# Transformer block with routed experts on one core: heads exchanged through DRAM in pairs, two sequences transposed on TensorE, small work moved to GpSimd, a written-out order of steps

## The chip, the cores and the metric

The kernel runs on one core of a Trainium2 chip. The metric is the device time of one execution in microseconds, lower is better. Three timed executions of the kernel before gave 1186.53, 1188.41 and 1190.04 us; the median, 1188.41 us, is its time. One execution was profiled; it took 1186.62 us, and the span from its first to its last instruction is 1184.9 us.

## The reference

The input is 16 sequences of 256 tokens with 256 channels, in float32, and one condition vector per sequence. The block is attention with 16 heads of 64 channels and then 8 experts; each expert takes the 512 tokens (of 4096) that give it the highest gate.

```python
shift = jax.nn.silu(t) @ W_ada.T + b_ada
h = _ln(x, ln1_g, ln1_b) + shift
qkv = (h @ Wqkv.T).reshape(b, n, 3, H, HD)
q = _ln(qkv[:, :, 0].transpose(0, 2, 1, 3), qn_g, qn_b)
k = _ln(qkv[:, :, 1].transpose(0, 2, 1, 3), kn_g, kn_b)
v = qkv[:, :, 2].transpose(0, 2, 1, 3)
attn = jax.nn.softmax(jnp.einsum('bhnd,bhmd->bhnm', q, k) / jnp.sqrt(jnp.float32(HD)), axis=-1)
o = jnp.einsum('bhnm,bhmd->bhnd', attn, v)
x = x + o.transpose(0, 2, 1, 3).reshape(b, n, H * HD) @ Wout.T
tok = x.reshape(-1, d)
gate = jax.nn.softmax(tok @ Wgate.T, axis=-1)
vals, idx = jax.lax.top_k(gate.T, k_cap)
g = _ln(tok[idx_flat], mlp_g, mlp_b).reshape(k_cap, E, d)
y = jax.nn.gelu(jnp.einsum('ked,ehd->keh', g, fc1s) + b1s, approximate=True)
y = (jnp.einsum('keh,edh->ked', y, fc2s) + b2s) * w[..., None]
tok = tok.at[idx_flat].add(y.reshape(-1, d))
```

## The kernel before

**Attention, per sequence.** The kernel is written as steps, small functions that each issue a few instructions on one engine. For every sequence b:

- `First` (L486) normalises x. VectorE takes the statistics (L471, L473) and adds eps (L475), GpSimd raises to the power -0.5 (L181, called `rsqrt`), VectorE applies it (L481). TensorE transposes the result (L505), ScalarE evicts it as hT (L513).
- `Group` (L527) makes 512 columns of q, k or v for 128 tokens: TensorE (L539, 8 groups of q and k and 4 of v per sequence), and for q and k the square on ScalarE (L552), the sum and the eps on VectorE (L556, L560), the power on GpSimd (L181), the scaling on VectorE (L572), four transposes on TensorE (L581) and the eviction on ScalarE (L593). v is copied by ScalarE (L548).
- `Quad` (L601) handles four heads: two pairs i, each with two heads j. `scores` (L614) writes the scores of a pair to PSUM, the two heads in the upper and lower half of TensorE's rows. Then come the maxima on VectorE (L621), the exponentials with their sums on ScalarE (L630), the reciprocal on VectorE (L637), the normalisation on GpSimd (L641). The probabilities must be transposed before the product with v. VectorE transposes blocks of 32x32 (`turn`, L651) into a tile `pb` for four heads; `away` (L659) writes this tile to DRAM in one transfer of 1 MB; `back` (L668) reads it with four transfers of 256 KB, each into 32 partitions, which completes the transposition. `product` (L679) multiplies with v for one pair, and ScalarE evicts both pairs (L690). `pb`, `blocks` (in DRAM) and `prT` have two buffers each.
- `Tail` (L693) projects half a sequence (L701), adds x and takes the statistics of the second normalisation (L708, L471 to L475), stores the token (L712), applies the normalisation (L481) and stores it for the experts (L722), transposes the token (L727) and computes the gate (L738, L744).

**Routing.** When all but the last sequence have their gates, the gates are turned (L803), and a loop of 30 steps finds for each expert the threshold of its first 256 tokens, bit by bit: VectorE compares and counts (L866), TensorE sums the counts over partitions (L875), VectorE decides on the bit (L881, L890). Then follow masks, running sums, places, the turn of the places (L932), their split (L943, L944), one-hot rows (L999 to L1002) and their matmuls into a list of tokens (L1010). GpSimd gathers these tokens (L1026), and the first expert job starts (L1035, L1042, L1054). The last sequence, number 15, is still being worked on meanwhile; its tokens join the second half of the experts' lists.

**Experts.** 16 jobs, each with 256 tokens of one expert: up (L1054), GELU (L1061), down (L1070), scaling (L1081) and a scatter that adds (L1087).

**What sets the order.** All engines work through their own queue in order, and the order in which steps are issued is found when the program is built. Each step has an engine, a duration, what it needs and makes, the tiles that it uses, and a place (`at`, L1098). `Plan.order` (L69 to L139) is a list scheduler: on each engine it takes, of the steps that could start, the one with the lowest place. The places are given by `PLACES` (for sequences 0, 1, 14 and 15, and one list for all others, L258) and `OTHERS` (L357). The exchange is two steps on SP: `away` and, when it has landed, `back`. The experts behind the first job are issued by a loop of their own (L1285), which the change leaves as it is.

```python
plan = Plan(dict(
    mm=3, sc=4, po=1, xs=5, hT=2, qT=2, kT=2, v=2, oT=2, xn=4, sq=2, ss=4, qk=3, nmax=8,
    sums=4, pr=5, pb=2, prT=2, blocks=2, tok=3, tn=2, tokT=2, pa=1, l1=4, l2=4,
))
```

Of the kernel before, what the change touches and what calls it, by code (L numbers as in the profile page):

```python
# [9 lines left out]
F32 = mybir.dt.float32  # L10
# [8 lines left out]
P = 128  # L19
# [25 lines left out]
class Plan:  # L45
# [4 lines left out]

    SWITCH = 0.1

# [9 lines left out]
    def move(self, k, places, base=0.0):  # L65
        for n, p in enumerate(places):
            self.steps[k + n] = (base + p,) + self.steps[k + n][1:]

    def order(self):  # L69
        steps = self.steps  # L70
        waits, after = [0] * len(steps), [[] for _ in steps]
        users, first = {}, {}
        for k, s in enumerate(steps):
            for need in s[4]:
                for m in self.makers[need]:
                    after[m].append(k)
                    waits[k] += 1
            for t in s[5]:
                users[t] = users.get(t, 0) + 1
                first[t] = min(first.get(t, s[0]), s[0])  # L80
        queue, before = {}, {}
        for t in sorted(first, key=lambda t: (first[t], t)):
            q = queue.setdefault(t[0], [])
            before[t] = (q[-1] if q else None, q[-self.bufs[t[0]]] if len(q) >= self.bufs[t[0]] else None)
            q.append(t)
        opened, seen, ready = set(), dict.fromkeys(users, 0.0), [0.0] * len(steps)
        engines = sorted({s[1] for s in steps})
        free, mode, could = dict.fromkeys(engines, 0.0), 0, {e: [] for e in engines}
        for k, s in enumerate(steps):
            if not waits[k]:  # L90
                could[s[1]].append(k)

        def since(k):
            at = ready[k]
            for t in steps[k][5]:
                if t not in opened:
                    last, old = before[t]
                    if (last and last not in opened and last not in steps[k][5]) or (old and users[old]):
                        return None
                    if old:  # L100
                        at = max(at, seen[old])
            return at

        now, begun = 0.0, []
        while any(could.values()):
            soonest = None
            for e in engines:
                best = None
                for k in could[e]:
                    at = since(k)  # L110
                    if at is None:
                        continue
                    at = max(at, free[e])
                    if at > now:
                        soonest = at if soonest is None else min(soonest, at)
                    elif best is None or steps[k][0] < steps[best][0]:
                        best = k
                if best is None:
                    continue
                place, _, took, _, _, tiles, new, lag = steps[best]  # L120
                could[e].remove(best)
                begun.append((now, best))
                if e == "PE" and new != mode:
                    took, mode = took + self.SWITCH, new
                free[e] = now + took
                for t in tiles:
                    opened.add(t)
                    users[t] -= 1
                    seen[t] = max(seen[t], free[e] + lag)
                for j in after[best]:  # L130
                    waits[j] -= 1
                    ready[j] = max(ready[j], free[e] + lag)
                    if not waits[j]:
                        could[steps[j][1]].append(j)
                soonest = now
            assert soonest is not None, "the steps wait for each other"
            now = soonest
        assert len(begun) == len(steps)
        return begun  # L139
# [3 lines left out]
def kernel(  # L143
# [83 lines left out]
    def make_others():  # L227
# [20 lines left out]

    PERIOD = 48.3
# [8 lines left out]
    PLACES = {  # L258
        0: (
            -1144.55, -164.36, -115.53, -130.99, -318.93, -203.16, -250.78, -275.49, -88.56,  # L260
            -92.44, -65.27, -85.65, -66.22, -65.85, -65.32, 12.14, -6.18, -116.86, -181.88,
            -226.33, -125.11, -66.56, 28.05, -105.91, -20.3, -102.65, -221.15, -75.09, 2.35,
            -80.49, 1.34, -67.49, -85.29, 6.61, 41.35, -62.52, -33.41, -103.77, 18.66, -30.22,
            54.18, 129.48, -13.42, -83.84, 39.96, -48.35, -19.59, -36.56, -17.89, -45.17, 55.43,
            -70.52, -11.75, -35.26, 18.2, 127.34, -40.65, 197.67, -41.87, 25.57, -34.78, 6.26,
            -0.72, -16.64, -24.42, -19.76, -33.5, 146.36, -15.21, -80.44, -121.15, 16.4, -39.26,
            141.09, 130.08, -22.71, 7.22, 19.47, -35, 26, -18.23, 114.81, -30.2, 29.23, -17.79,
            38.44, -19.99, 169.58, 80.02, 70.31, -8.6, 150.94, -2.15, 56.48, 101.61, -24.78,
            -6.1, 29.81, -75.75, -44.1, -91.93, -42.35, 8.4, 56.38, -74.75, 9.88, -96.01, 81.36,
            4.1, -11.15, -69.31, 111.09, -81.61, -79.47, 132.37, -55.21, 0.19, -6.58, 10.81,  # L270
            -17.63, -89.05, -107.92, -85.01, 55.81, 73.89, -3.1, 47.74, 73.13, -1.31, 11.3,
            -4.77, -7.89, 119.67, 92.55, 13.36, 18.97, 19.3, 0.26, 98.83, 99.7, 5.08, 90.2,
            98.25, 89.81, 28.34, 13.88, -25.95, 96.99, 23.08, 24.48, 165.57, 95.49, 17.49,
            25.97, 340.13, 17.81, 30.6, 82.65, 76.24, 137.46, 26.87, 119.95, 28.51, 62.39,
            98.03, 29.11, 80.48, 33.67, 134.77, 55.75, 148.81, 19.6, 184.91, 184.91, 71.13,
            145.9, 172.26, -1.27, 65.12, 94.09, 77.65, 61.8, 129.73, 115.28, 77.3, 197, 137.64,
            83.55, 49.39, 91.96, 309.57, 84.45, 103.71,
        ),
        1: (
            -1099.37, -54.3, -64.13, -49.72, 71.37, -53.23, -29.87, -97.99, -83.01, -35.49,  # L280
            -46.75, -34.18, 81.89, -9.83, -37.19, 36.64, -62.82, 55.44, -65.48, -20.12, -47.55,
            -31.78, -47.55, -26.5, -51.81, -65.03, 0.47, 13.43, -46.75, -17.66, -38.8, -69.23,
            -71.58, 29.14, 26.88, -56, -43.27, -44.63, 17.07, -13.08, 26.91, 4.19, 10.21,
            -26.32, 70.91, -27.78, -19.98, -4.95, -12.76, -18.52, 56.95, -24.15, 33.02, -10.4,
            -14.8, 156.65, -25.28, 57.31, -18.9, -26.29, -16.56, -10.04, -7.87, -9.89, -16.41,
            19.91, -19.2, -7.41, 17.97, 72.84, -26.36, 1.28, -2.29, 247.68, 32.65, 5.1, 57.03,
            13.72, 64.3, 1.04, 25.24, 113.13, 73.57, 11.96, 44.14, 13.22, 7.46, 193.37, 89.15,
            25.45, 6.95, 78.59, 27.38, 82.69, 48.92, 27.8, 15.94, 20.2, -8.51, -6.59, 81.43,
            162.24, -3.77, 171.23, -7.27, 83.73, -2.31, 16.51, 10.99, -6.84, 2.75, 0.93, 116.67,
            47.85, 133.75, 4.98, 82.62, 123.39, 75.52, 59.15, 47.91, -25.4, 28.45, 153.76, 17.7,  # L290
            122.51, 20, 152.23, 14.52, 8.47, 137.08, 80.87, 51.01, 31.66, 134.83, 94.03, 23.05,
            126.07, 25.97, 99.38, 24.04, 64.78, 151.81, 126.94, 18.1, 166.1, 24.05, 47.47,
            129.86, 33.28, 68.61, 32.17, 28.96, 32.46, 270.75, 32.53, 67.18, 73.71, 15.97,
            43.31, 38.83, 226.09, 38.38, 44.84, 49.78, 71.7, 36.68, 123.74, 79.99, 76.02,
            102.24, 32.47, 43.7, 280.07, 70.72, 73.86, 167.32, 118.25, 62.67, 75.97, 178.87,
            46.5, 263.88, 75.76, 77.93, 71.3, 272.62, 159.42, 99, 76.57, 183.69, 106.19, 54.29,
        ),
        7: (
            191.51, -163.95, -123.74, -35.99, -95.07, -16.18, -24, -78.96, 25.94, -55.05, 8.08,
            -53.5, -64.73, -0.18, -46.06, 23.75, -54.52, -16.62, -53.05, -52.69, -42.2, 57.54,  # L300
            -48.11, 6.09, -51.7, 54.34, 45.68, -40.43, -29.34, -38.29, 100.8, -47.57, -35.63,
            20.29, -6.51, -31.42, 49.06, 18.7, -41.88, -24.12, 16.51, 24.92, 85.5, -32.56,
# [81 lines left out]
    if True:  # L384
# [80 lines left out]
        class Norm:  # L465
# [11 lines left out]
            def power(self):  # L477
                rsqrt(self.rs[:, 1:2], self.rs[:, 0:1])
# [48 lines left out]
        class Group:  # L527
# [36 lines left out]
            def power(self):  # L564
                rsqrt(self.ss[:, 1, :], self.ss[:, 0, :])
# [811 lines left out]
```

## Time and profile before

| what | value |
|---|---|
| median of three executions | 1188.41 us |
| the profiled execution: its time, its span | 1186.62 us, 1184.9 us |
| busy: TensorE matmul, VectorE, ScalarE, GpSimd | 92%, 68%, 50%, 49% of the span |
| mean granted TensorE clock | 0.965 |
| start of the 30 counts of the first routing (L875), last count | 859.6 us, 907.0 us |
| first block of the first expert job (L1054) | 930.2 us |
| end of TensorE's work | about 1174 us |

The profile lists instructions by engine, kernel line and operation, with the tiles' names as out<-in, a count, the busy time and the mean duration. "PEld" is the weight load of a matmul, which overlaps other matmuls. A number in brackets in the timeline is the idle time of the engine before that row, with what ended it; consecutive equal instructions of a row are merged (x8 is eight instructions). A float32 matmul appears as two instructions. The ends of matmuls are modelled, so for TensorE the distance from start to start says more than the busy time. Times of the timeline count from the span's start.

### The profile page before, as it was taken

What the parts mean: (1) busy time and instruction counts of PE and PEld (TensorE: products, weight loads), DVE (VectorE), ACT (ScalarE), POOL (GpSimd) and SP (SyncE); (2) the same over time, 40 slices, a digit from 0 to 9 for tenths busy, and PEclk for the clock granted to TensorE, in tenths of its full rate; (3) what the DMA queues carried; (4) which work ended last, traced back from release to release, by engine and by line L of the source; (5) the groups of instructions that cost most, each with busy time, mean ns of one, the idle gap of its engine ahead of it and who ended that gap; (6) DMA issues with size and microseconds to landing.
All of it is one profiled execution on the core that took longest, in us unless ns stands there. A gap on an engine that the chain in (4) does not pass through costs nothing. (4 is left out here: it accounts for less than half of the span.)

```text
span 1184.9 us, 17925 instructions
## 1 busy us (share of the span) xinstructions
PE 1089.6 (92%) x5787; PEld 715.9 (60%) x5787; DVE 800.6 (68%) x2364; ACT 593.9 (50%) x1661; POOL 574.8 (49%) x805
## 2 busy tenths in 40 slices
PE   7899999999999999999999999999845799999996
PEld 4444546565565656555565655556624688888885
DVE  6776667676867767676866767578657478755540
ACT  2675556656565666565555655556501333233331
POOL 2665555566656546555655565456400233333332
PEclk8998999999999999999999999999966899999998
DMA  5147356656664647746665664746850366666661
GB/s 197 52 133 219 124 140 204 196 155 169 195 193 136 204 125 222 193 150 177 174 201 165 178 186 138 198 146 207 249 170 10 109 184 183 187 187 187 186 184 22
DMA packets 92813, 196.53 MB, mean 166 GB/s; under 512 B 9008, under 2 KB 45104, under 8 KB 84528
## 3 DMA queue, kind: packets, MB, share of 16 engines
q1 hardware_dynamic: 82944, 183.27, 52.4%
q0 software_dynamic: 6144, 8.39, 3.8%
q10 hardware_dynamic: 3632, 3.74, 0.9%
q8 instruction: 46, 0.75, 0.3%
q14 instruction: 47, 0.39, 0.1%
HBM read 115.67 MB, written 79.69 MB: 165 GB/s over the span
## 5 line engine op out<-in xcount | busy, mean ns | idle before, releaser
L539 PE MATMUL pm<-wq,hT 128*128 128x512 f32 x768 | 363.8, 610 | 5.5 <-DVE wq L461 3.5
L181 POOL TENSOR_TENSOR ss<-ss,neghalf 128x8 f32<-128x8 f32 x128 | 210.0, 1645 | 222.3 <-DVE ss L560 191.0
L641 POOL TENSOR_SCALAR pr<-pr,sums 128x256 f32<-128x256 f32 x512 | 236.3, 479 | 90.7 <-DVE sums L637 85.1
L630 ACT ACTIVATE pr<-sc,nmax 128x256 f32<-128x256 f32 x512 | 236.7, 477 | 44.8 <-DVE nmax L621 41.6
L539 PEld LDWEIGHTS pm<-wq,hT 128*128 128x128 f32 x768 | 139.0, 194 | 145.7 <-issue 125.4
L621 DVE TENSOR_REDUCE nmax<-sc 128x2 f32<-128x512 f32 x256 | 165.4, 677 | 56.2 <-PE sc L614 56.0
L651 DVE STREAM_TRANSPOSE pb<-pr 128x512 f32<-128x512 f32 x256 | 171.7, 690 | 17.1 <-POOL pr L641 16.5
L679 PE MATMUL po<-prT,v 128*64 128x256 f32 x1024 | 135.0, 401 | 38.3 <-DMA prT<-blocks 34.5
L614 PE MATMUL sc<-kT,qT 64*128 64x256 f32 x1024 | 142.2, 400 | 0.1
L679 PEld LDWEIGHTS po<-prT,v 128*64 128x64 f32 x1024 | 73.0, 141 | 105.8 <-issue 33.9
L556 DVE TENSOR_REDUCE ss<-sq 128x8 f32<-128x512 f32 x128 | 86.6, 676 | 56.7 <-ACT sq L552 56.0
L701 PE MATMUL pw<-wo,oT 128*128 128x256 f32 x512 | 120.6, 391 | 0.0
L1054 PE MATMUL ph<-xT,w 128*128 128x256 f32 x512 | 118.3, 384 | 0.0
L614 PEld LDWEIGHTS sc<-kT,qT 64*128 64x128 f32 x1024 | 90.1, 187 | 45.9 <-issue 33.6
L1070 PE MATMUL py<-w,hid 128*128 128x256 f32 x512 | 116.6, 380 | 0.0
L701 PEld LDWEIGHTS pw<-wo,oT 128*128 128x128 f32 x512 | 99.2, 196 | 25.6 <-issue 9.4
L552 ACT ACTIVATE sq<-pm 128x512 f32<-128x512 f32 x128 | 76.7, 600 | 74.4 <-PE pm L539 70.3
L1087 POOL DMA_INDIRECT out<-y,idx x32 | 51.1, 1597 | 120.7 <-DVE y L1081 57.5
L572 DVE TENSOR_TENSOR qk<-pm,ss 128x512 f32<-128x512 f32 x128 | 87.3, 684 | 29.8 <-POOL ss L181 29.3
L630 ACT ACTIVATION_READ_ACCUMULATOR pr<-sc,nmax 128x1 f32 x512 | 107.4, 210 | 0.0
L1054 PEld LDWEIGHTS ph<-xT,w 128*128 128x128 f32 x512 | 96.0, 191 | 13.0
L1070 PEld LDWEIGHTS py<-w,hid 128*128 128x128 f32 x512 | 95.5, 190 | 12.7
(133 smaller groups left out, 1034.0 us busy)
## 6 DMA issues: line engine op xcount, KB each, us to landing
blocks<-pb SPq DMA_DIRECT2D x64, 1024.0 KB, 4.3
prT<-blocks SPq DMA_DIRECT2D x256, 256.0 KB, 6.5
w<-in_fc2T SPq DMA_DIRECT2D x16, 1024.0 KB, 5.5
w<-in_fc1T SPq DMA_DIRECT2D x16, 1024.0 KB, 8.3
out<-tok SPq DMA_DIRECT2D x32, 128.0 KB, 5.0
xn_dram<-tn SPq DMA_DIRECT2D x32, 128.0 KB, 4.1
xs<-in_x SPq DMA_DIRECT2D x12, 256.0 KB, 3.0
b<-in_b2s SPq DMA_DIRECT2D x16, 128.0 KB, 8.4
```

The lines of the kernel that those rows point to most:

```text
L181: nc.gpsimd.tensor_tensor(dst, src, neghalf[:, : src.shape[1]], ALU.pow)
L539: nc.tensor.matmul(self.pm, hTs[self.b][:, c, bass.ts(self.t, P)], wq[:, c, bass.ts(self.g, GW)], start=(c == 0), stop=(c == DC - 1),)
L572: engine.tensor_tensor(self.qk.rearrange("p (h d) -> p h d", d=HD), src.rearrange("p (h d) -> p h d", d=HD), self.ss[:, 1, :].unsqueeze(2) ...
L614: nc.tensor.matmul(self.sc[i, j][:, t, :], qTs[self.b][rows, hp, bass.ts(t, P)], kTs[self.b][rows, hp, :], start=True, stop=True,)
L621: nc.vector.tensor_reduce(self.nmax[i, j], self.sc[i, j], AX.X, ALU.max, negate=True)
L630: nc.scalar.activation(self.pr[i, j][:, t, :], self.sc[i, j][:, t, :], AF.Exp, bias=self.nmax[i, j][:, t : t + 1], scale=1.0, accum_out=se ...
L641: nc.gpsimd.tensor_scalar(self.pr[i, j][:, t, :], self.pr[i, j][:, t, :], self.sums[i][:, 1, j, t : t + 1], 1.0, ALU.mult, ALU.mult,)
L651: nc.vector.transpose(self.pb[:, :, :, 2 * i + j].rearrange("p k c t n -> p t c k n"), self.pr[i, j].rearrange("p t (c k m) -> p t c k m", ...
L679: nc.tensor.matmul(self.po[j * HD : (j + 1) * HD, i, :], vs[self.b][:, c, bass.ts(4 * self.d + 2 * i + j, HD)], self.prT[:, :, c, 2 * i + ...
L701: nc.tensor.matmul(self.pw, oTs[self.b][:, hp // 2, self.t, hp % 2, :], wo[:, hp, :], start=(hp == 0), stop=(hp == HP - 1),)
L1054: nc.tensor.matmul(self.ph[f], self.w1[:, c, bass.ts(f, P)], self.xT[:, c, :], start=(c == 0), stop=(c == DC - 1),)
L1070: nc.tensor.matmul(self.py[i], self.hid[:, f, bass.ts(i, P)], self.w2[:, f, :], start=(f == 0), stop=(f == FC - 1),)
```

## The change

Five things change together.

1. The exchange through DRAM is done for two heads (one pair i) at a time: `pb`, `blocks` and `prT` belong to a pair, with 3, 4 and 4 buffers. `away` writes 512 KB, and each of the four transfers of `back` reads 128 KB, in pieces of 256 floats where there were 512.
2. Sequences 0 and 15 (`DIRECT`) do not go through DRAM: TensorE transposes the probabilities of a head in four 128x128 blocks into a PSUM tile (tag `sc`), and ScalarE copies them to `prT`. VectorE's block transposes fall away for these two.
3. eps is added on GpSimd instead of VectorE (both normalisations, and q and k), and both normalisations are applied on GpSimd.
4. The first job's one-hot rows, 30 in all, go to VectorE, GpSimd and ScalarE as 15, 10 and 5, where they went to VectorE and ScalarE as 20 and 10. `pr` has six buffers instead of five.
5. The scheduler is removed. `PLACES` is now one list with a number for each of the 3669 steps, in the order of the `at` calls, and steps are issued in ascending order of it.

```diff
-    def order(self):
-        steps = self.steps
...
+    def order(self, places):
+        assert len(places) == len(self.steps)
+        return sorted(range(len(places)), key=lambda k: (places[k], k))
...
+    DIRECT = (0, B - 1)
+    PRB = 6
...
+    PLACES = (
+        0, 0, 3.3, 5.22, 3.75, 4.72, 4.42, 7.47, 0.23, 0.53, 9.39, 8, 20.02, 16.58, 12.59, 11.2,
...
-                nc.vector.tensor_scalar_add(self.rs[:, 0:1], self.mv[:, 1:2], EPS)
 
             def power(self):
+                nc.gpsimd.tensor_scalar(
+                    self.rs[:, 0:1], self.mv[:, 1:2], EPS, 1.0, ALU.add, ALU.mult
+                )
                 rsqrt(self.rs[:, 1:2], self.rs[:, 0:1])
 
             def apply(self, dst):
-                nc.vector.tensor_scalar(
+                nc.gpsimd.tensor_scalar(
                     dst, self.src, self.mv[:, 0:1], self.rs[:, 1:2], ALU.subtract, ALU.mult
                 )
...
-                nc.vector.tensor_scalar(
+
+            def power(self):
+                nc.gpsimd.tensor_scalar(
                     self.ss[:, 0, :], self.ss[:, 0, :], 1.0 / HD, EPS, ALU.mult, ALU.add
                 )
-
-            def power(self):
                 rsqrt(self.ss[:, 1, :], self.ss[:, 0, :])
...
-            def away(self):
-
-                self.blocks = dram.tile([QB, SQ, QB, GW], F32, tag="blocks", bufs=2, name="blocks")
+            def away(self, i):
+
+                self.blocks[i] = dram.tile([QB, SQ, QB, N], F32, tag="blocks", bufs=4, name="blocks")
                 nc.sync.dma_start(
-                    self.blocks.rearrange("k m q n -> (k m) (q n)"),
-                    self.pb.rearrange("p q c h t n -> p (q c h t n)"),
-                )
...
+            def turned(self, i):
+                if i not in self.prT:
+                    self.prT[i] = work.tile([P, 2 * TB * N], F32, tag="prT", bufs=4, name="prT")
+                return self.prT[i]
+
+            def back(self, i):
+
+                prT = self.turned(i).rearrange("p (k n) -> p k n", k=QB)
                 for q in range(QB):
                     nc.sync.dma_start(
...
+                        prT[bass.ts(q, SQ)], self.blocks[i][:, :, q].rearrange("k m n -> m k n")
+                    )
+
+            def transposes(self, i, j):
+                self.pp[i, j] = ps.tile([P, TB, N], F32, tag="sc", bufs=4, name="pp")
+                for c in range(TB):
+                    for t in range(TB):
+                        nc.tensor.transpose(
+                            self.pp[i, j][:, c, bass.ts(t, P)],
+                            self.pr[i, j][:, t, bass.ts(c, P)], ident,
+                        )
+
+            def copy(self, i, j):
+                prT = self.turned(i).rearrange("p (h c n) -> p h c n", h=2, c=TB)
+                nc.scalar.copy(prT[:, j], self.pp[i, j])
...
+                    elif engine is nc.gpsimd:
+                        nc.gpsimd.tensor_scalar(
+                            self.oh[:, t, :], lane1, place, 1.0, ALU.is_equal, ALU.mult
+                        )
...
-            sums=4, pr=5, pb=2, prT=2, blocks=2, tok=3, tn=2, tokT=2, pa=1, l1=4, l2=4,
+            sums=4, pr=PRB, pb=3, prT=4, blocks=4, tok=3, tn=2, tokT=2, pa=1, l1=4, l2=4,
...
+            who = "DPADPD" if n == 0 else "DDDDDD"
...
-        for _, k in plan.order():
+        for k in plan.order(PLACES):
             plan.steps[k][3]()
```

What the list says, read off by sorting it. The places of a step on SP or another engine count against TensorE's only through what it needs. On TensorE, behind the gate of the second half of sequence 14, the order is: two products of sequence 15, two of its transposes (a transposes step is one head), the turn of the gates, and then, between the counts of the routing loop (numbered from 29 down to 0):

```
turn of the gates | transposes, scores | count 29 | product, scores, product | 28 | transposes | 27 | - | 26 |
scores, transposes, product | 25 | transposes | 24 | - | 23 | transposes, transposes | 22 |
product, transposes | 21 | transposes, product | 20 | product | 19 | - | 18 | projection | 17 |
projection | 16 | token transposes, gate, token transposes | 15 | gate | 14 | ... | 0
```

Before, the profile has six of the eight products of sequence 15, two of its v groups (L539) and its two projections in or next to this loop; the second projection starts at 912.1 us, behind it. A piece of SP's new order (sequence, then quad and pair as two digits): away 7.11, back 7.11, away 7.20, away 7.21, back 7.20, away 7.30, back 7.21, two stores, away 8.00, away 7.31, a load, a store, away 8.01, back 7.31, back 7.30, a store, back 8.00, back 8.01, away 8.10, back 8.10. Each `back` is four issues.

## The prediction

> **What bounds the kernel now.** I began with the page's 40 slices, to see where TensorE is not full.
>
> ```profile
> PE   7899999999999999999999999999845799999996
> PEclk8998999999999999999999999999966899999998
> ...
> q1 hardware_dynamic: 82944, 183.27, 52.4%
> ...
> q10 hardware_dynamic: 3632, 3.74, 0.9%
> ```
>
> TensorE is nearly full except in the first slices and in three near 70%. The table of busy time by stage puts numbers on this (columns: span, then PE, PEld, DVE, ACT and POOL busy with instructions, TensorE clock, DMA share, GB/s).
>
> ```profile
> 0.00:100.00 100.00, 83.97 (x341) 46.78 (x341) 70.05 (x154) 51.14 (x136) 50.63 (x72) 0.90 0.45 138
> ...
> 182.00:707.00 525.00, 503.13 (x2560) 298.42 (x2560) 380.35 (x849) 314.83 (x921) 304.93 (x455) 1.00 0.63 178
> ...
> 853.00:930.00 77.00, 37.72 (x197) 24.02 (x194) 45.87 (x240) 12.04 (x37) 12.58 (x24) 0.68 0.43 131
> 930.00:1174.00 244.00, 243.63 (x1565) 213.73 (x1563) 140.82 (x766) 80.34 (x165) 80.19 (x66) 1.00 0.55 161
> ```
>
> From 182 to 707 us the projection of a sequence (L701) starts ten times, so a sequence takes 52.5 us. DVE is busy 72%, ACT 60%, POOL 58%, the DMA engines 63%: TensorE is the bound, and only its own work and its own waits matter. Its work, start to start in the timeline of one period: 12 q/k/v blocks at 1.72, 8 blocks of q/k transposes at about 0.5, 8 of scores at 1.06, 4 pairs of products at 1.88, 2 projections at 3.5, the rest 2.1; together 49.8 us. So some 2.7 us of a period are waits. Next I read the waits of TensorE from 125 to 850 us, then the timeline of one period, where they stand at two places:
>
> ```profile
> PE po L679 <- DMA prT<-blocks: 22.4, 19, 1.8
> ```
>
> ```profile
> 430.42 1.95 PE L679 MATMUL po<-prT,v 128*64 128x256 f32 x16 [1.42 <-DMA prT<-blocks]
> ...
> 434.95 1.08 PE L679 MATMUL po<-prT,v 128*64 128x256 f32 x8 [0.93 <-DMA prT<-blocks]
> ```
>
> The product waits for probabilities that come back from DRAM. In the start the same wait costs more, as the clock falls too; at the end it holds up the routing loop (TensorE's timeline, then VectorE's):
>
> ```profile
> 89.97 3.68 PE L679 MATMUL po<-prT,v 128*64 128x256 f32 x16 [3.17 <-DMA prT<-blocks]
> 94.40 3.68 PE L679 MATMUL po<-prT,v 128*64 128x256 f32 x16 [0.76 <-ACT oT L690]
> ...
> 880.74 1.97 PE L679 MATMUL po<-prT,v 128*64 128x256 f32 x8 [5.20 <-DMA prT<-blocks]
> ...
> 895.41 6.48 PE L701 MATMUL pw<-wo,oT 128*128 128x256 f32 x16
> ```
>
> ```profile
> 859.85 0.22 DVE L890 SCALAR_TENSOR_TENSOR cand<-pc,drop,keep 128x1 f32<-128x1 f32 x1 [3.79 <-PE pc L875]
> ...
> 882.87 0.22 DVE L890 SCALAR_TENSOR_TENSOR cand<-pc,drop,keep 128x1 f32<-128x1 f32 x1 [6.39 <-PE pc L875]
> ```
>
> The loop of 30 counts runs from 856 to 907 us. Undisturbed it needs 1.00 us a turn (counts at 864.61 and 865.61), in which TensorE is idle 0.84. It is late where its count stands in TensorE's queue behind a block of sequence 15. From 930 us TensorE is full; the change does not touch that stage.
>
> **The sum**, against the profiled execution (1186.6 us; the median of the three runs is 1.8 above).
>
> *Steady stretch.* Four heads make one 1 MB transfer out (4.3 us to landing) and four of 256 KB back (6.5), and the way out waits for the last of four block transposes. For the wait at 430.42 above, SP's timeline has the way out issued at 416.92 and the ways back from 422.74 on: 13.5 us from the way out to the product. With two heads, the way out waits for two transposes, and there are three, four and four buffers of half the size instead of two. From the scores to the second transpose the rows give two maxima (0.68), two exponentials (1.0), the reciprocal (0.17), two normalisations (0.94) and two transposes (0.69), 6.8 us and with queueing some 10; the exchange adds at most 4.3 + 4 x 0.43 + 6.5 = 12.5. In the list at least 27 us of TensorE work stand between the scores of two heads and their product in sequences 2 to 13 (36 now, but for four heads). Waits before products from 125 to 850 us are 24.6 us by the waits view (22.4, and 1.4 and 0.8 named for ACT), with 0.07 more at each of 21 starts: 26. I take 21 out and leave 5 for new waits. Bounds: +5 (none of the old ones goes and the new ones come on top) and -26. **-21**.
>
> *Sequence 0.* No way through DRAM: the waits of 3.17 and 0.76 go, and the two products of 3.68 at a low clock come back to 1.88: 7.5 us. TensorE also waits 6.2 us there for VectorE's scaling; VectorE loses 16 transposes of 0.69 (11 us) in this stretch, so I take half, 3. Bounds: 1 (next sentence) and 19 (all 16 us that TensorE is idle in the first 100, and 3.5 of the low clock). **-10.5**. ACT pays with 16 copies like L690's (0.59, 9.4 us) where it is busy 51%; that hides, and if it did not, the products would wait for up to 9 us: 10.5 - 9.4 = 1.
>
> *Added TensorE work.* Each of 32 heads is four 128x128 transposes, a block like L581's (0.49). For sequence 0: 16 x 0.49 = 7.8. For sequence 15, ten of 16 stand in the routing window (below), six before: 2.9. Two v blocks of sequence 15 (3.4) now stand ahead of the window, three score blocks (3.2) move into it. The list changes between the score or product form and others 14 times more (335 against 321), at 0.09 each: 1.3. **+12.2**.
>
> *Routing window.* Now: last gate of sequence 14 at 851.4, first expert block at 930.2, 78.8 us. After: 4.6 to the first count, 30 turns of 1.00, plus what the blocks between two counts exceed 0.84. In the list these are 2.96 (product, scores, product), 2.5, 0.98, 1.44, 1.44, 0.95, twice 3.5 (projections) and 1.1; the excess is 10.9, and 0.7 before the turn of the gates: 46.2, against 55.6 now. Full clock is assumed; TensorE is busier here than now, but if the clock fell to half as in 895.41, the blocks would double and 10 us come back. Behind the last count nothing of sequence 15 is left, and a third of the one-hots goes to GpSimd: ten at 0.54 (the nearest row is L207's, 128x128) and 0.9 for the gives, 7.0 to the list, against 9.3 now. That is 2.3 less; bounds +1 and -4. **-11.7**.
>
> *At nothing.* The eps operations (192) and both normalisations (64) go to GpSimd. The trace has no eps there; by its rows a small operation takes 0.23 (L786, 128x16) to 0.56 (L181, 128x1), so 44 to 108 us in all, I take 44, the plain arithmetic; 64 x 0.48 for applying (L641's form) makes 75. GpSimd rises from 58% to 66%, VectorE falls by 62 us. A chain gets 0.2 longer, covered by the blocks that stand between a q/k block and its transposes; without that cover it is 0.2 on each of 128 transposes, 26 us. SP issues 40 instead of 20 exchange transfers a sequence at 0.43 each: 17 of 50 us. SP works in order: a way back that waits for its way out holds the next way out and the stores behind it, and only products and the reuse of token tiles wait for those.
>
> *Packets.* The way back now moves 1 KB instead of 2 KB at a time. The trace's packet records have 2 KB on this path at 152 ns (19.5 us per sequence and engine) and 1 KB elsewhere at 46 to 54; the page's q10 row is 47. Bounds for a 1 KB packet are thus 46 and 152; I take 76, half of the same path's row, so the engines carry what they carry now (32.4 us of a period).
>
> "DMA: Bandwidth & Descriptors" in the Trainium skill (Anatomy of one DMA; Bandwidth) speaks against the change: a transfer costs a fixed 2 us plus its bytes at 436 GB/s, and should be batched to 1 MB or more. By it the way out is 4.4 us (the row: 4.3) and a half of it 3.2, so two in a row take 2.0 longer than one; over 56 quads that is 112 us of an in-order queue, which would make the time 1289 (1186.6 - 10 for the other terms + 112) if TensorE stood behind all of it. The row of TensorE's waits says that it stands behind 24.6 us in all.
>
> Sum: -21 - 10.5 + 12.2 - 11.7 = -31, so 1155.6 in the profiled execution, which lies 1.8 below the median; I give **1156**.
>
> **Rivals.**
> *More than that* (1140): each term at its better end, -26 - 19 + 12.2 - 13.4 = -46. For it: the first two stand on waits that rows name. Against: a new order always brings some wait.
>
> *The waits only move* (1180): two thirds of the steady 21 stay, because SP's queue is in order and has twice the transfers, and the window's clock falls, +10: -31 + 14 + 10 = -7. The change then does not do what it says. For it: SP already waits 104.8 us for the way out to land (L668). Against: in the list other issues stand between most ways out and their ways back.
>
> *Slower* (1207): 1 KB packets cost as much as 2 KB ones. Then the way back takes 4096 x 152 / 16 = 39 us per sequence instead of 19.5, and the engines carry 52 us. No row of the stages has them over 0.63; at 0.95 a sequence takes 54.7, and 14 x 2.2 = 31 come on top, the steady 21 are not won, the rest gives 10. It decides from about 147 ns: then 12.9 + 37.6 = 50.5 us of transfers need a period of 53.2, which eats those 10. For it: 2 KB takes 152 on this path and 84 on q10, so something other than bytes counts. Against: 8 KB takes 317, which goes by bytes.
>
> **How the numbers follow.** Forecast 0.55, more 0.15, waits move 0.20, slower 0.10. The second rival is faster by 7 us in its middle, and 0.3% (about what a measurement can tell from no change) is 3.6, so 0.03 of it lies within; of the slower case 0.01. Faster 0.55 + 0.15 + 0.17 = 0.87, the same 0.04, slower 0.09. The range from 1134 to 1182 takes in the first three cases to their middles and beyond, and leaves out the slower one and the far half of the second rival.
>
> **What would show it.** Right: waits of L679 for DMA under 5 us from 125 to 850; a period near 50; counts of the routing loop about 1 us apart after the projections; no wait of sequence 0's products for DMA. Wrong: 1 KB packets over 130 ns and a DMA share over 0.85; q/k transposes (L581) waiting for GpSimd's chain; the loop longer than 50 us.

## The result and the profile after

After: 1144.41 us (median of four, 1144.07 to 1145.36) against 1188.34 us for before on the same chip; the ratio is 0.9632, interval 0.9615 to 0.9649. The profiled execution took 1144.71 us, its span is 1143.0 us: 41.9 us less than the profiled execution of before, where the prediction had 31 less (its 1156 is the profiled execution's figure, 1155.6; with the 1.8 that it names itself the median's would be 1157).

First the page of the kernel after: the 40 slices of TensorE and of its clock, then the exchange's queue (packets, MB, share of 16 engines).

```profile
PE   6999999999999999999999999999961999999996
...
PEclk7999999999999999999999999999985899999999
...
q1 hardware_dynamic: 117504, 166.51, 45.6%
```

TensorE is now full from the second slice on, one hole is left, the routing window. The queue moves more packets in a smaller share of time, and 9% fewer bytes (166.51 MB instead of 183.27), as two sequences no longer pass through it. The table of busy time by stage of the kernel after (span, then PE, PEld, DVE, ACT and POOL, clock, DMA share, GB/s):

```profile
0.00:100.00 100.00, 89.58 (x408) 50.49 (x408) 52.30 (x103) 57.64 (x146) 68.60 (x108) 0.93 0.20 68
...
180.00:684.00 504.00, 501.15 (x2570) 295.21 (x2568) 345.96 (x685) 313.94 (x922) 378.94 (x616) 1.00 0.58 182
...
822.00:888.00 66.00, 33.57 (x263) 24.33 (x262) 46.45 (x239) 17.99 (x52) 25.59 (x44) 0.72 0.14 47
888.00:1133.00 245.00, 244.60 (x1547) 214.09 (x1547) 140.09 (x762) 79.59 (x162) 80.79 (x66) 0.99 0.55 161
```

Ten sequences take 503.0 us from projection to projection, 50.3 each instead of 52.5; GpSimd is busy 75% of that, the DMA engines 0.58 instead of 0.63. The waits of TensorE from 125 to 822 us in the kernel after, complete (us in total, times, longest):

```profile
PE pq L712 <- DVE qk L703: 2.8, 7, 0.5
PE po L831 <- DVE gates L900: 1.1, 2, 0.8
```

Of the 22.4 us in which products waited for DMA nothing is left. In TensorE's timeline of the window (after), the counts are L1031, the projections of sequence 15 L857, the first expert block L1214:

```profile
824.40 0.18 PE L1031 MATMUL pc<-cnt,twice 128*128 128x1 bf16 x1
...
841.08 3.70 PE L857 MATMUL pw<-wo,oT 128*128 128x256 f32 x16
844.62 0.17 PE L1031 MATMUL pc<-cnt,twice 128*128 128x1 bf16 x1
...
865.27 0.16 PE L1031 MATMUL pc<-cnt,twice 128*128 128x1 bf16 x1 [0.84 <-DVE reach L1022]
...
887.59 2.93 PE L1214 MATMUL ph<-xT,w 128*128 128x256 f32 x6
```

No scores or products of sequence 15 wait for their data between the counts; the loop takes 40.9 us from first to last count instead of 47.4. So what the prediction named as signs of being right is there: no product waits for DMA anywhere in the trace of after, the period is 50.3, and behind the second projection and the two gates the counts stand 1.00 apart (864.27, 865.27). Of its signs of being wrong the trace has one in small: the q/k transposes wait 2.8 us.

For the rest I cut every trace at the same four points of TensorE: first projection of sequence 1, first projection of sequence 11, turn of the gates, first expert block. "Start" ends at the first, then come "ten periods", "run-down" and "window"; what follows, to the end of TensorE's work, is 245 to 247 us in every run. TensorE's work in a stage is the sum of its instructions at the start-to-start interval that each form has where nothing waits (0.429 us for 512 columns, 0.2155 for 256, 0.1075 for a score or product, 0.109 for a transpose, 0.09 per change of form; smaller forms likewise); the remainder is stall. It holds more than waits: 19.1 us in the ten periods of after, where the waits view names 2.8. It also holds what TensorE loses where its granted clock is below 1 (0.93 before and 0.96 after up to some 180 us, 0.68 and 0.72 in the window, by the stage rows). So only its changes are read.

| | start | ten periods | run-down | window |
|---|---|---|---|---|
| before: length, work | 182.4, 139.5 | 524.9, 484.4 | 146.2, 134.9 | 76.7, 20.6 |
| after: length, work | 180.8, 153.1 | 503.0, 483.9 | 138.7, 133.6 | 65.0, 24.7 |
| change of the stall | -15.2 | -21.4 | -6.2 | -15.8 |

The work grows by 15.9 us, the stall falls by 58.6, and the first expert block starts 42.6 earlier (930.2, 887.6).

### The profile page after: what moved, and what is told of

It reads as the page before. It is cut to its first block, busy times and chain, and to the rows that moved or that the text cites. A ratio compares the mean times of both kernels' runs of the same rounds, so it can differ in the third digit from the quotient of the medians.

```text
span 1143.0 us, 18776 instructions
## 1 busy us (share of the span) xinstructions
PE 1086.2 (95%) x5915; PEld 714.2 (62%) x5915; DVE 727.8 (64%) x2071; ACT 606.3 (53%) x1683; POOL 701.7 (61%) x1071
## 3 DMA queue, kind: packets, MB, share of 16 engines
q1 hardware_dynamic: 117504, 166.51, 45.6%
## 5 line engine op out<-in xcount | busy, mean ns | idle before, releaser
L772 POOL TENSOR_SCALAR pr<-pr,sums 128x256 f32<-128x256 f32 x512 | 235.6, 478 | 63.6 <-DVE sums L768 47.4
L670 PEld LDWEIGHTS pm<-wq,hT 128*128 128x128 f32 x768 | 134.9, 192 | 123.0 <-issue 113.5
L782 DVE STREAM_TRANSPOSE pb<-pr 128x512 f32<-128x512 f32 x224 | 150.4, 693 | 29.4 <-POOL pr L772 28.2
L831 PE MATMUL po<-prT,v 128*64 128x256 f32 x1024 | 131.9, 389 | 1.1 <-DVE gates L900 1.1
L1214 PE MATMUL ph<-xT,w 128*128 128x256 f32 x512 | 119.8, 388 | 0.0
L857 PE MATMUL pw<-wo,oT 128*128 128x256 f32 x512 | 117.2, 382 | 0.0
L687 DVE TENSOR_REDUCE ss<-sq 128x8 f32<-128x512 f32 x128 | 86.3, 674 | 47.4 <-ACT sq L683 47.4
L857 PEld LDWEIGHTS pw<-wo,oT 128*128 128x128 f32 x512 | 95.8, 190 | 24.0 <-issue 11.2
L831 PEld LDWEIGHTS po<-prT,v 128*64 128x64 f32 x1024 | 65.2, 136 | 68.9 <-issue 34.1
L1214 PEld LDWEIGHTS ph<-xT,w 128*128 128x128 f32 x512 | 97.1, 193 | 13.6
L1221 ACT ACTIVATE hid<-ph,vec 128x256 f32<-128x256 f32 x128 | 60.3, 473 | 85.0 <-PE ph L1214 76.7
```

The costliest lines, as they stand in the source:

```text
L670: nc.tensor.matmul(self.pm, hTs[self.b][:, c, bass.ts(self.t, P)], wq[:, c, bass.ts(self.g, GW)], start=(c == 0), stop=(c == DC - 1),)
L772: nc.gpsimd.tensor_scalar(self.pr[i, j][:, t, :], self.pr[i, j][:, t, :], self.sums[i][:, 1, j, t : t + 1], 1.0, ALU.mult, ALU.mult,)
L782: nc.vector.transpose(self.pb[i][:, :, :, j].rearrange("p k c t n -> p t c k n"), self.pr[i, j].rearrange("p t (c k m) -> p t c k m", c=TB ...
L831: nc.tensor.matmul(self.po[j * HD : (j + 1) * HD, i, :], vs[self.b][:, c, bass.ts(4 * self.d + 2 * i + j, HD)], prT[:, j, c] if self.b in ...
L857: nc.tensor.matmul(self.pw, oTs[self.b][:, hp // 2, self.t, hp % 2, :], wo[:, hp, :], start=(hp == 0), stop=(hp == HP - 1),)
L1214: nc.tensor.matmul(self.ph[f], self.w1[:, c, bass.ts(f, P)], self.xT[:, c, :], start=(c == 0), stop=(c == DC - 1),)
```

## The experiments

**Theories.** W, that of the prediction: products waited for the exchange; a chain of two heads is shorter, and sequences 0 and 15 have none. O: the new order does it, whatever the exchange. V: GpSimd relieves VectorE. Where a run has a new order, it is made by the list scheduler of before with the places of after as its priorities; with nothing else changed this gives the order of after, instruction for instruction. The scheduler also weighs the exchange: where that changes, the same places give another order. Counting consecutive equal instructions of TensorE as one block, 604 of the 676 blocks of before come in the same sequence in e6, 678 of the 739 of e12 in e7, and 724 of the 774 of after in e1 (longest common sequence). So no run changes the exchange alone; e3, e5 and e11 keep their kernel's order. e6, e7 and e12 all have the sixth `pr` tile, which was not tried by itself; e1, e7 and e9 have one buffer for a tile of the expert jobs (`bw`), and their time behind the window is no longer. Times are medians, and ratios are to before on the same chip (1187 to 1189 us).

| run | what | start | ten periods | run-down | window | time | ratio, interval |
|---|---|---|---|---|---|---|---|
| e5 | before, no product waits | 176.0 | 501.9 | 145.0 | 68.9 | 1147.6 | 0.9654, 0.9634 to 0.9674 |
| e6 | before, two heads | 181.9 | 508.0 | 158.2 | 65.5 | 1171.0 | 0.985, 0.9826 to 0.9875 |
| e7 | before's operations, new order | 186.4 | 508.7 | 139.7 | 79.6 | 1168.7 | 0.9837, 0.9818 to 0.9856 |
| e12 | two heads and new order | 177.2 | 499.9 | 138.0 | 70.0 | 1142.2 | 0.9622, 0.9583 to 0.9662 |
| e1 | after, four heads | 186.6 | 517.9 | 139.8 | 65.3 | 1165.8 | 0.9825, 0.98 to 0.985 |
| e9 | e1, eps on VectorE | 186.3 | 505.4 | 139.4 | 65.7 | 1153.8 | 0.9717, 0.9686 to 0.9747 |
| e3 | after, eps on VectorE | 183.1 | 500.0 | 138.3 | 65.8 | 1142.6 | 0.9622, 0.9598 to 0.9646 |
| e11 | before, eps on GpSimd | 194.6 | 525.5 | 146.2 | 76.3 | 1199.3 | 1.011, 1.0067 to 1.0152 |
| e10 | the same, order made anew from before's places | 196.0 | 539.6 | 160.4 | 73.9 | 1226.5 | 1.0322, 1.0276 to 1.0368 |
| e2 | after, nothing direct | 179.2 | 503.3 | 138.5 | 72.4 | 1149.4 | 0.9687, 0.9663 to 0.971 |
| e4 | after, one-hots not on GpSimd | 179.1 | 503.0 | 138.7 | 60.3 | 1139.2 | 0.9611, 0.9587 to 0.9636 |
| e8 | the best of it | 177.8 | 499.9 | 138.3 | 60.7 | 1134.3 | 0.9548, 0.9532 to 0.9564 |

**e5: the price of the waits.** The kernel before, with products that read a tile that is always there. The exchange still runs; the run leaves out the probabilities in the products, so it computes something else and only prices the waits:

```diff
-                            self.prT[:, :, c, 2 * i + j, :],
+                            wq[:, 0, :N],
```

> The kernel before, its order unchanged, with the products of all sequences reading a weight tile that is always there; the exchange still runs, but its result is not used (left out: the probabilities in the products). This prices the waits before products. By the waits view of before: 26 us in the steady stretch, some 8 in the start, 5 in the routing window, so 1187.6 - 39 = 1148 to 1150. By start to start (32 in the steady stretch instead of 26): 1142 to 1144. If a wait only moves to the next resource (q/k chain, PSUM), 1160 or more.

Measured 1147.6, just under the 1148 to 1150 of the waits view. By stage, 6.4 go in the start, 23.0 in the ten periods, 1.2 in the run-down and 7.8 in the window, 38.4 in all. The waits view, with 24.6 for the stretch from 125 to 850, had priced the steady part rightly: 23.0 and 1.2 make 24.2. At before's order, then, these waits are worth nearly as much as the whole change gained.

**e6, e7, e12: exchange and order, each alone and both.** e6 changes in the kernel before

```diff
-            sums=4, pr=5, pb=2, prT=2, blocks=2, tok=3, tn=2, tokT=2, pa=1, l1=4, l2=4,
+            sums=4, pr=PRB, pb=3, prT=4, blocks=4, tok=3, tn=2, tokT=2, pa=1, l1=4, l2=4,
...
-                    self.pb = work.tile([P, QB, TB, 4, TB, SQ], F32, tag="pb", bufs=2, name="pb")
+                    self.pb[i] = work.tile([P, QB, TB, 2, TB, SQ], F32, tag="pb", bufs=3, name="pb")
```

with `away` and `back` per pair (and six `pr` tiles); the scheduler of before makes the order from before's places. e7 takes after's places and keeps before's operations. e12 has both.

> The kernel before with the exchange by two heads (3, 4 and 4 buffers of half the size) and nothing else changed; the order is made by the planner of before from before's places. Theory W (the shorter chain is the gain): the steady waits go, 21 to 32 us, so 1156 to 1167. Theory O (the order sets the waits): within 4 us of 1187.6, since the places were made for four heads.

> All operations of before (four heads in one transfer, sequences 0 and 15 through DRAM, eps and normalisations on VectorE, one-hots on VectorE and ScalarE) in an order made by the planner from the places of after. If the parts add up: 1144 + 21 (four heads) + 5 (no direct) - 2 (eps) = 1168, between 1163 and 1173, which leaves some 20 us below before to the new places. Theory W in its pure form (only the exchange counts): 1180 or more. Theory O in its pure form: 1150 or less.

> The exchange by two heads and the order from after's places, all other operations as before (eps and normalisations on VectorE, no direct sequences, one-hots on VectorE and ScalarE). It fills the square with before (1188), two heads alone (1171) and order alone (1168.7). If both remove the same waits, less than their sum of 37 us is left: 1152 to 1160. If each does its own, 1188 - 37 = 1151 or less; from the run without direct sequences (1149.4), less 2 for eps, it should be 1147.

Measured: two heads without the new places 17.8 less than before (1188.8 there; at 1171.0 above W's range of 1156 to 1167), the new places without two heads 20.1 less, both 46.0 less (1188.2 there; 1142.2, where the runs had led to 1147). So neither W nor O holds in its pure form, and the guess that both only remove the same waits falls too: together they bring more than the sum (by 8 us, where the three intervals leave some 6 of doubt). The stages show how. In the ten periods they overlap: 16.9 and 16.2 apart, 25.0 together. There each takes all of before's 20.5 us of product waits for DMA away. TensorE's waits from 125 to 850 us, the largest group of e6, then the two largest of e7:

```profile
PE pl L769 <- ACT tokT L764: 5.5, 4, 3.8
```

```profile
PE pq L784 <- DVE qk L775: 5.1, 6, 2.2
PE po L903 <- DMA prT<-blocks: 4.8, 1, 4.8
```

The 4.8 us stand in the window, behind the turn of the gates. At both ends each alone wins next to nothing, and both together do (in one profiled execution each): the start changes by -0.5 (two heads), +4.0 (order) and -5.2 (both), run-down and window together by +0.8, -3.6 and -14.9. In e7 two products between the counts wait 4.8 and 3.7 us for DMA and the loop takes 58.0 us; in e6 the window is 11.2 shorter, but the run-down 12.0 longer. What in the old places makes that run-down longer was not tried.

**e1 and e9: four heads again.** In the kernel after, both pairs use one `pb`, `prT` and `blocks` of four heads (two buffers each) and

```diff
-                    if b not in DIRECT:
+                    if b not in DIRECT and i:
```

> The kernel after, with the exchange put back to four heads in one transfer (two buffers each), and the order made anew by the planner of before from the places of after. Theory W (products no longer wait for the exchange, because a chain of two heads is shorter): the waits before products come back in the steady stretch, TensorE's period rises from 50.3 to 52 or more, and the time is 1166 to 1177, 21 (by the waits of before) to 32 us (by start to start) more than after's 1144. Theory O (the new order alone, whatever the exchange): the time stays within 4 us of 1144. Theory V (relief of VectorE by GpSimd): no change either, as VectorE has the same work here.

> The run with the exchange put back to four heads (1165.8), with the eps operations and normalisations on VectorE and its order otherwise unchanged. It asks why TensorE waited there 9.5 us for scaled q/k and not for DMA. If GpSimd's longer chain (eps, power) is what is late once the cover of the earlier products is gone, those waits go and ten periods fall from 517.9 to 509, so 1157 +- 3. If the longer way of four heads itself pushes the blocks together, the time stays at 1164 to 1167, as the same edit was worth 2 us in the kernel after.

Measured 1165.8 for e1, 21.4 more than after, at the lower end of W's range, but the wait is another one than W named. TensorE's waits in the ten periods of e1, the two largest groups:

```profile
PE pq L786 <- DVE qk L777: 9.2, 7, 3.0
PE po L905 <- DVE gates L974: 2.4, 1, 2.4
```

No product waits for DMA in e1: the order made for the longer exchange covers it, and q/k is late instead. One such wait of e1, in the timelines of VectorE, GpSimd and TensorE, one fence each:

```profile
309.08 0.43 DVE L674 BATCH_NORM_STATS2 st<-xs 128x6 f32<-128x256 f32 x1 [1.90 <-DMA xs<-in_x]
...
313.63 0.69 DVE L777 TENSOR_TENSOR qk<-pm,ss 128x512 f32<-128x512 f32 x1 [2.72 <-POOL ss L177]
```

```profile
309.82 0.19 POOL L680 TENSOR_SCALAR rs<-mv 128x1 f32<-128x1 f32 x1 [3.57 <-DVE mv L676]
...
311.95 1.65 POOL L177 TENSOR_TENSOR ss<-ss,neghalf 128x8 f32<-128x8 f32 x1
```

```profile
314.47 0.63 PE L786 MATMUL pq<-ident,qk 128*128 128x128 f32 x4 [1.75 <-DVE qk L777]
```

An eps operation stands at the head of GpSimd's queue for 3.57 us, of which VectorE's wait for a late load of x makes 1.90; the power for q/k stands behind it, then VectorE's scaling, then TensorE. e9 puts eps and normalisations back on VectorE and takes 12.0 us out of e1, all of it in the ten periods (517.9 to 505.4), with the order of e1; its wait for q/k there is 2.0 instead of 9.2. That is just below the expected 1157 +- 3; the rival (no change) falls. The wait at the head of the queue is not by itself what goes: in the ten periods of e9 the power of a normalisation waits there for VectorE 49.0 us in 27 waits, where e1's eps waits 30.4 in 18. What goes is work: GpSimd is busy 60% of them instead of 73%. Whether the eps operations or the normalisations of 1.22 us are what is too much was not tried apart. In the kernel after the same move is worth 3.0 us in the ten periods, in e1 12.5: the cover that hides GpSimd's longer chain comes with the shorter exchange and the order made for it.

**e3, e11, e10: eps and normalisations.** The edit of e3, in the kernel after (and the eps of q and k likewise); e11 is its reverse in the kernel before:

```diff
-                nc.gpsimd.tensor_scalar(
-                    self.rs[:, 0:1], self.mv[:, 1:2], EPS, 1.0, ALU.add, ALU.mult
-                )
+                nc.vector.tensor_scalar_add(self.rs[:, 0:1], self.mv[:, 1:2], EPS)
...
-                nc.gpsimd.tensor_scalar(
+                nc.vector.tensor_scalar(
                     dst, self.src, self.mv[:, 0:1], self.rs[:, 1:2], ALU.subtract, ALU.mult
```

> The kernel after with the eps operations and both normalisations back on VectorE, and nothing else moved (the order of the other instructions is after's). Theories W and O: off TensorE's path, 1144 within 4 us; VectorE rises by some 60 us, GpSimd falls by more than that. Theory V: the gain came from VectorE's queue, so waits for VectorE come up in TensorE's list and the time is 1155 or more.

> The kernel before with the eps operations and normalisations on GpSimd and the order of every other instruction as it was (the run before this one had a new order from the planner). If GpSimd's longer chain alone made the 39 us, they come again: 1215 to 1235. If the planner's other order made them, the time is 1186 to 1196, as the same move cost 2 us in the kernel after.

> The kernel before with only the eps operations and normalisations moved to GpSimd, order made by the planner of before from before's places. Theory V (relief of VectorE): 10 to 25 us faster. Theory W (off the path, TensorE waits for the exchange): within 6 us of before, 1182 to 1194, and slower rather than faster, as the chain to a q/k transpose grows by an operation on GpSimd.

V falls. In the kernel after the move is worth nothing (1142.6 back on VectorE; the ratios' intervals overlap): its ten periods cost 3.0 more with it, its start 2.3 less. In the kernel before it costs 11.0 us with the order untouched, 12.2 of it in the start and 0.6 in the ten periods. TensorE's waits in the start, e11 first, then before:

```profile
PE pq L583 <- DVE qk L574: 13.2, 9, 3.7
...
PE ph L507 <- POOL xn L483: 2.6, 2, 1.9
```

```profile
PE pq L581 <- DVE qk L572: 6.4, 9, 2.1
...
PE ph L505 <- DVE xn L481: 0.7, 1, 0.7
```

e10, the same with a new order, is 39 us slower than before, where V had 10 to 25 less and W at most 6 more. Neither expectation for e11 (39 again, or nothing) was met: of e10's 39 us the chain makes 11, and the order that the scheduler made for it the other 28. What in that order costs them stays open.

**e2: nothing direct.**

```diff
-    DIRECT = (0, B - 1)
+    DIRECT = ()
```

> The kernel after, with sequences 0 and 15 sent through DRAM by two heads like the others; order made anew by the same planner from the places of after. Theory W: 16 us of transposes leave TensorE, but the waits of the start (10.5) and the excess of the routing window (9.4) come back, so the time is 1144 + 4, between 1140 and 1156, and products of sequence 0 wait for DMA again. Theory O: the transposes were pure cost, the order hides the exchange in the start and at the end too: 1144 - 16 = 1128 to 1134. Theory V: VectorE gets 32 block transposes back, 11 us of them in the start: 1144 to 1155, with TensorE waiting for VectorE instead of DMA.

Measured 1149.4, 5.0 more, inside the ranges of W and V; O, with 1134 or less, falls. The window is 7.4 longer, with the loop at 47.7, and no product of sequence 15 waits for DMA there either. Three counts come 2.6, 0.8 and 0.5 us later than a free turn of 1.00 would have them, while VectorE's queue holds block transposes and maxima again. And from 839.93 to 850.55 no count runs, as three pairs' products and a projection stand before the next. The first of these products takes 1.98 us, where most take 1.08 in after: TensorE's granted clock is 0.50 from 833 to 846.4, and 1.00 in after from 824 to 848, where the transposes keep it busy. So the direct way of sequence 15 pays in the loop. The start is not longer (179.2 against 180.8, and 179.1 in e4, which has the same start as after). No product of sequence 0 waits for DMA in e2: with two heads and the new order, the direct way of sequence 0 does not pay. With eps on VectorE it even costs some 5 us: the start is 183.1 in e3, and 177.2 and 177.8 in e12 and e8, which lack it.

**e4 and e8: a better version.**

```diff
-            who = "DPADPD" if n == 0 else "DDDDDD"
+            who = "DDADDD" if n == 0 else "DDDDDD"
```

and in the order the gives of the first job go ahead on GpSimd, two groups of the second job's one-hots behind the first's. e8 has this, eps and normalisations on VectorE, and `DIRECT = (B - 1,)`.

> The kernel after, with ten of the first job's 30 one-hots moved from GpSimd (0.77 us each there, 7.7 in all, with the gives behind them) to VectorE (0.19 each), and the gives first on GpSimd. If GpSimd's chain of 8.6 us between split and list ends last, as the trace of after reads, the list matmuls start 3.5 to 4.5 us earlier: 1140 to 1141. If the gather or the weights end last, the time stays within 1 us of 1144.

> The kernel after with three steps of the change taken back or mended, as the runs so far price them: the first job's one-hots on VectorE and ScalarE only (-5), eps and normalisations on VectorE (-2), sequence 0 through DRAM by two heads and only sequence 15 on TensorE (-1.6, from the start of the run without direct sequences). Sum 1136, between 1133 and 1139. If the last two were chance, 1139.

GpSimd's queue behind the split of the places in the kernel after, and the list matmuls that wait for it (TensorE, after, then e4):

```profile
871.52 7.74 POOL L1158 TENSOR_SCALAR oh<-lane,partf 128x128 bf16<-128x128 bf16 x10 [19.72 <-DVE partf L1100]
879.24 0.44 POOL L1138 TENSOR_TENSOR give<-vals,partf 128x150 bf16<-128x150 bf16 x1
879.75 0.45 POOL L1143 TENSOR_TENSOR give<-vals,give 128x150 bf16<-128x150 bf16 x1
```

```profile
880.25 0.94 PE L1170 MATMUL pls<-give,oh 128*128 128x10 bf16 x30 [9.75 <-POOL give L1143]
```

```profile
872.64 1.92 PE L1244 MATMUL pls<-give,oh 128*128 128x10 bf16 x30 [3.89 <-DVE oh L1236]
```

From the last count (865.27 and 863.51) to the first expert block it is 22.3 us in after and 17.6 in e4. e4's 1139.2 lies 0.8 below its expectation, and the intervals of its ratio and of after's overlap, so the times alone would not show a gain. This stretch does: it is 22.2 to 22.8 in the five runs with one-hots on GpSimd (after, e1, e2, e3, e9) and 17.6 and 17.7 in e4 and e8. The one-hots and the order of the gives were not tried apart. e8 adds the three: 1134.3 us, as expected (1133 to 1139), ratio 0.9548, below after (0.9632) with intervals apart. It beats both kernels.

## Why the prediction was right, and where it was not

Right in sign and range, and the wait that it named went: no product waits for DMA any more. But the shorter exchange is not the only thing that takes this wait away; in the ten periods the new order with four heads does it too (e7), and the prediction gave the order nothing. Some 11 us of gain were missing, nearly all in the stalls: predicted -47.9 (-21, -10.5, and in the window -11.7 and the 4.7 of work that moved into it by the prediction's figures: ten transposes and three score blocks in, two v blocks out), measured -58.6. The added work was nearly right: outside the window 12.2 predicted and 11.8 measured, in it 4.7 and 4.1.

- **The steady stretch, "I take 21 out and leave 5 for new waits"**: the term mis-sized. The stall of ten periods and run-down falls by 27.6. e5 shows that the 26 read from the waits view were the price, 24.2 in these two stages; but after has 3.9 us of waits there in all, and the run-down lost 5.0 more than e5's. A new order was counted as a risk only ("a new order always brings some wait"). e7 shows that the new places are a gain of 20 us without two heads.
- **Sequence 0, -10.5**: the step failed in its cause. The stall of the start fell by 15.2, but e2, without the direct way, has a start as short as after's. Product waits were worth 6.4 there (e5). The rest is order: the start takes 13.6 us more work than before, of which the transposes are 7.8, in a time 1.6 shorter; work of later sequences now stands where TensorE idled. The 7.8 us bought nothing.
- **Routing window, -11.7**: met in sum (76.7 to 65.0), by luck, as its parts missed. Behind the last count 0.9 came instead of 2.3, since a one-hot on GpSimd takes 0.77 us and not 0.54, as L207's row suggested. The loop gave 6.5, and from the turn of the gates to the first count 4.2 went. The assumption of a full clock held: 1.00 from 824 to 848, where before has 0.57 under its projection at 895.41. e2 puts 7.4 of the window down to the direct way of sequence 15.
- **Eps "at nothing"**: it held for the kernel after, on a cover that the sum named. GpSimd rose to 75%, further than the 66% of the sum (by its own 75 us it should have said 67), because the normalisation takes 1.22 us and not L641's 0.48. Without the cover it costs 11 (e11) or 12 (e9), less than the 26 given.
- **Packets**: 1 KB packets of this queue, five in six of them on the exchange's way back, take 59 ns in the mean of the ten periods, not 76, so the rival "slower", which needed 147, fell; the DMA share went down.

The Trainium skill's "DMA: Bandwidth & Descriptors" (Anatomy of one DMA; Bandwidth), which would have smaller transfers pay a fixed 2 us each, gave an estimate of 1289 by that reading; the page measured this on transfers that GpSimd issues, and the exchange is issued by SP. The run shows no such loss: twice as many transfers per sequence, no wait of TensorE for any of them, and two heads with the old places (e6) are a gain.

## What to carry to other kernels

Here the waits view was right about what a removed wait is worth (e5). Price a new order as a term of its own, from the idle time of the stages that it can fill. Splitting a transfer can pay where its latency, not its bytes, is late. Moving small work to another engine that works in order was free only behind a cover: ask what stands behind it in that queue, and look up its duration there in a row of the same operands.

## What the runs showed that I had not expected

The normalisation, subtract and multiply by two per-partition operands, takes three times as long on GpSimd as on VectorE. Groups from 300 to 600 us, GpSimd in the kernel after (busy, mean ns), then VectorE in the kernel before:

```profile
L772 POOL TENSOR_SCALAR pr<-pr,sums 128x256 f32<-128x256 f32 x192 | 88.4, 478 | 23.7 <-DVE sums L768 19.6
...
L612 POOL TENSOR_SCALAR xn<-xs,mv,rs 128x256 f32<-128x256 f32 x12 | 14.5, 1216 | 0.3
```

```profile
L481 DVE TENSOR_SCALAR xn<-xs,mv,rs 128x256 f32<-128x256 f32 x13 | 4.8, 405 | 0.0
```

With one such operand and a constant (L772) the same shape takes 478 ns on GpSimd, so instruction and shape do not fix the time. It does not hang on what VectorE does beside it: the 32 normalisations of tokens (tn) in after take 1.21 to 1.23 us each. The bf16 one-hot of 128x128 takes 0.77 us on GpSimd, and 0.17 on VectorE (30 in 5.16 us in e4). Here company counts: while VectorE makes its own one-hots in after (until 876.2), those of GpSimd take 0.79 to 0.89 each, then 0.71, and VectorE's take 0.19. "GPSIMD Engine Reference" in the Trainium skill (4.1 Engine selection) has operations with one input tensor at roughly line rate on GpSimd; these two take three and more than four times what they take on VectorE. A packet of 1 KB took 59 ns in the mean in the exchange's queue, where one of 2 KB on the way back had taken 152.
